# Layer 2 window attention: weights loaded first, exponentials behind the copies, routing in slots 12 to 18

## The chip, the cores and the metric

The kernel runs on one core of one Trainium2 chip. The metric is the time of one execution on the device in microseconds (us), the median of several runs; less is better. The engines are TensorE (PE, matrix products; PEld is its weight load), VectorE (DVE), ScalarE (ACT), GpSimd (POOL) and SyncE (SP, which here only asks for transfers).

## The reference

Input: two images of 256 channels and 32 x 32 pixels, float32. Four layers, each an attention and, in layers 2 and 3, a mixture of experts. Layers 0 and 1 are attentions over the pixels. Cut to the part that matters here:

```python
# layer 2, tokens t: (2, 1024, 256)
t = t + window_attention(layernorm(t))      # rolled by 32, windows of 64 tokens, 8 heads of 32:
#   qkv = x @ w_qkv.T + b_qkv; sim = q @ k.T * 32**-0.5 + rel_pos; probs = softmax(sim)
#   out = (probs @ v) @ w_out.T + b_out
# then a mixture of 8 experts, top 2 of each token, on x = layernorm(t):
logits = x @ Wr + br
top_p, top_idx = top_k(softmax(logits), 2); weights = top_p / top_p.sum()
xn = layernorm(x); xe = xn * ln_g[e] + ln_b[e]      # x is normalised a second time
y_e = gelu(xe @ W1[e] + b1[e]) @ W2[e] + b2[e]
t = t + sum over the two experts of weights * y_e
# layer 3: an additive attention (tanh) over each image, then experts again
```

## The kernel before

`Stack.run` does layer 0, layer 1, then builds `Late` (constants, small weights, the code of the experts), then `window_attention`, then `Late.run`. Tokens lie in `t`, 16 tiles of 128 tokens by 256; tiles 0 to 7 are image 0, tiles 8 to 15 image 1. A tile holds two windows.

`window_attention` loads `w_qkv`, `w_out` and the biases after `Late.__init__` has put its own loads into the same SP queue, normalises image 0 (`normed(0)`: inverse root, eight scalings, transposes into `uT`), and then runs a loop of 20 slots. In slot i stand, in this order, `value(i)` (v of the tile), `scores(i)` (32 small products, softmax on DVE, ACT and POOL, result in `probs`), `turn(i-2)` (transposes of `probs`, two copies to `ptT` on ACT), one of four parts of the q and k projection of a later group of four tiles (`project`), a step of `normed(1)` in the first six slots, `sums(i-3)` (probabilities times v), `output(i-4)` (times `w_out`, added to `t`), and from slot 10 on three steps of `route`. `route` is the generator `late.dispatch(2, 0)`: twice `gate` (statistics, normalisation, transposes and router product of four tiles), then `Late.route` (softmax, the two best experts, counts, slots of the sorted list, rows of the expert weights), a second normalisation of the eight tiles (`norm`), 16 scatters of the tokens into `slots_in` by POOL's indirect transfers (L1161), and `shift` (the experts' second bias times the weights of the token, added to `t`). What the loop has not used up of it, `Late.run` continues as step `D20`.

The loop is written inside

```python
with tc.manual_schedule(engines={engines.PE, engines.Activation}):
```

so PE and ACT work in the order of the loop's lines; DVE, POOL and SP are ordered by the framework's scheduler by readiness and program order. Products go to PSUM tiles of one pool with three buffers (`misc`, tag `ps_mm`): `ps_va`, two of `ps_pt`, `ps_qk`, `ps_wo` in each slot; a buffer is free when its reader has drained it.

Where the change touches it: the exponential L884 stands on ACT inside `scores(i)`, so ahead of the copies of `turn(i-2)` L909; v is drained by DVE with its bias (L901), q by ACT (L858), k by DVE (L860); `output` makes `y` on DVE (L935) and adds it to `t` on POOL (L936).

`Late.run` interleaves named steps by a plan: for each the steps that must have been issued before it, a planned time and the distance between its pieces. `E20` and `E21` are the experts of the two images, `D21` the routing of image 1, `C20` the collection of the results, `A0` the additive attention of image 0. `E20` needs `D20`: it loads its tokens (`xr`, L1371) from `slots_in`, and the weights of the expert (`ew`, `fetch`, L1322) by POOL's indirect transfers.

Of the kernel before, what the change touches and what calls it, by code (L numbers as in the profile page):

```python
# [27 lines left out]
P = 128  # L28
# [41 lines left out]
class Stack:  # L70
# [707 lines left out]
    def window_attention(self, t, late):  # L778
# [7 lines left out]
        with ExitStack() as ctx:  # L786
# [35 lines left out]
            uT, q, k, v, pT, o = {}, {}, {}, {}, {}, {}  # L822
# [22 lines left out]
            def project(g, part):  # L845
# [11 lines left out]
                if part < CC:  # L857
                    nc.scalar.activation(to, ps, AF.Identity, bias=b_qk[:, part : part + 1])  # L858
                else:
                    nc.vector.tensor_scalar(to, ps, b_qk[:, part : part + 1], None, ALU.add)  # L860

            def scores(i):
# [21 lines left out]
                nc.scalar.activation(l, l, AF.Exp)  # L884
# [8 lines left out]
            def value(i):  # L893
# [7 lines left out]
                nc.vector.tensor_tensor(v[i], ps, b_v, ALU.add)  # L901
# [25 lines left out]
            def output(i):  # L927
# [13 lines left out]
            engines = mybir.EngineType  # L941
            with tc.manual_schedule(engines={engines.PE, engines.Activation}):
                for part in range(2 * CC):
                    project(0, part)
                for i in range(NT + 4):
# [3 lines left out]
                    if 2 <= i < NT + 2:  # L949
                        turn(i - 2)  # L950
                    if i + 4 < NT:
                        project(i // 4 + 1, i % 4)
                    if i < 6:
                        next(other, None)
                    if 3 <= i < NT + 3:
                        sums(i - 3)
                    if 4 <= i:
                        output(i - 4)
                    if i >= 10:
                        for _ in range(3):  # L960
                            next(route, None)
# [28 lines left out]
class Late:  # L990
# [3 lines left out]
    def __init__(self, ctx, stack, t):  # L994
# [4 lines left out]
        self.early = ctx.enter_context(tc.tile_pool(name="early_sb", bufs=2))  # L999
        self.made = {}  # L1000
# [3 lines left out]
        tl = lambda name, shape: self.w.tile(shape, F32, name=name)  # L1004
        self.wr = {l: stack.load(self.w, n, "(c p) e -> p c e", p=P) for l, n in ((2, "wr"), (3, "gate_w"))}
# [138 lines left out]
    def dispatch(self, *key, done=0):  # L1144
# [3 lines left out]
        n = len(tokens)  # L1148
        for half in range(done, n // 4):
# [6 lines left out]
        nc = self.nc  # L1156
# [13 lines left out]
        if l == 2:  # L1170
            yield from self.shift(*key)
# [532 lines left out]
    def run(self, route):  # L1704
# [132 lines left out]
```

## Time and profile before

| what | us |
|---|---|
| median of 3 runs (2844.81 to 2851.49) | 2851.44 |
| the profiled execution | 2887.74 |
| its span, first to last instruction | 2886.0 |
| PE busy / DVE / ACT / POOL in the span | 2635.3 / 1944.8 / 1815.6 / 1235.5 |
| end of layer 1's last product | 1623.2 |
| first q/k product of layer 2 (L852) | 1640.5 |
| first and last scatter (L1161) start | 1779.6, 1801.6 |
| first product of the experts (L1404) starts | 1810.6 |

The profile is of one execution, which took somewhat longer than the runs timed without it; times inside it are from its first instruction. A line of the timeline gives start, duration, engine, line of the kernel, operation, `out<-in`, shapes, count, and in brackets how long the engine stood idle before and what ended that. A line of the waits gives who waited for whom, us in total, times, and the longest. In the table by stages each engine's busy time is followed by its number of instructions; PEclk is the clock granted to PE as a share of full speed.

### The profile page before, as it was taken

To read this page: it belongs to the slowest core of one execution; us is meant where nothing else is said; L and a number is where in the kernel's file an instruction comes from. 1 tells how busy PE (TensorE), PEld (TensorE's weight loads), DVE (VectorE), ACT (ScalarE), POOL (GpSimd) and SP (SyncE) were. 2 spreads that over 40 slices of the span, in tenths; PEclk is the share of its full clock that TensorE was granted. 3 is DMA by queue.
4 is the path that set the end of the run, shared out by engine and by line. 5 is a ranking of instruction groups with operands and counts; after the bars stand their busy time and mean duration, and the time that the engine had idled before them with its cause. 6 is when DMAs were issued, how large, how long until landed. Compare 5 with 4: busy or idle time off the path is not lost. (4 is left out here: it accounts for less than half of the span.)

```text
span 2886.0 us, 77396 instructions
## 1 busy us (share of the span) xinstructions
PE 2635.3 (91%) x32006; PEld 1643.6 (57%) x32006; DVE 1944.8 (67%) x3642; ACT 1815.6 (63%) x2685; POOL 1235.5 (43%) x1302
## 2 busy tenths in 40 slices
PE   7899999999999998799999686999999988999987
PEld 3455555555555555555555454998666632465676
DVE  5999999999999999478789577633422343134242
ACT  2777777778777777255555231211699878889722
POOL 4877777777777775001111134244111112102242
PEclk9999999999999999899999897999999999899998
DMA  3000000000000000111010100543222001322354
GB/s 133 3 3 3 3 3 3 3 3 3 3 3 3 3 3 3 49 31 28 11 31 9 28 1 30 202 134 99 68 81 76 16 24 35 128 67 87 116 166 125
DMA packets 180577, 131.39 MB, mean 46 GB/s; under 512 B 130992, under 2 KB 162368, under 8 KB 173056
## 3 DMA queue, kind: packets, MB, share of 16 engines
q0 software_dynamic: 29232, 81.71, 8.5%
q1 hardware_dynamic: 147824, 44.25, 6.8%
q8 instruction: 251, 4.11, 0.6%
q10 hardware_dynamic: 3168, 0.48, 0.1%
q14 instruction: 102, 0.84, 0.1%
HBM read 181.24 MB, written 29.49 MB: 73 GB/s over the span
## 5 line engine op out<-in xcount | busy, mean ns | idle before, releaser
L188 ACT ACTIVATE sc<-sc,sa_shift 128x1024 f32<-128x1024 f32 x512 | 584.5, 1144 | 153.1 <-DMA sa_shift<-sa_min 150.8
L201 DVE STREAM_TRANSPOSE wt<-sc 128x1024 f32<-128x1024 f32 x512 | 601.5, 1207 | 0.2 <-ACT sc L188 0.2
L1622 ACT ACTIVATE th<-kT,qb 128x1024 f32<-128x1024 f32 x512 | 540.4, 1135 | 66.2 <-PE ps_e L1631 40.1
L211 PEld LDWEIGHTS ps_o<-wt,v 128*64 128x64 f32 x8192 | 444.4, 137 | 188.9 <-issue 106.2
L143 PE MATMUL ps_s<-kT,qT 64*32 64x512 f32 x8192 | 527.6, 595 | 18.0 <-ACT sc L153 17.2
L211 PE MATMUL ps_o<-wt,v 128*64 128x128 f32 x8192 | 505.0, 276 | 26.8 <-DVE oT L372 26.7
L166 POOL TENSOR_TENSOR fold<-sc 128x512 f32<-128x512 f32 x256 | 329.2, 1286 | 195.9 <-ACT sc L153 177.0
L168 POOL TENSOR_TENSOR fold<-sc,fold 128x512 f32<-128x512 f32 x256 | 328.4, 1283 | 21.4
L153 ACT COPY sc<-ps_s 128x1024 f32<-128x1024 f32 x256 | 256.0, 1000 | 111.0 <-PE ps_s L143 57.1
L1631 PE MATMUL ps_e<-th,pick 128*32 128x512 f32 x2048 | 305.7, 613 | 20.5 <-ACT th L1622 9.3
L1404 PEld LDWEIGHTS ps_h<-xe,ew 128*128 128x128 f32 x2320 | 278.1, 194 | 63.6 <-issue 39.0
L150 DVE TENSOR_SCALAR_CACHE_REDUCE sc<-ps_s 128x1024 f32<-128x1024 f32 x256 | 304.3, 1189 | 7.1 <-PE ps_s L143 6.6
L1404 PE MATMUL ps_h<-xe,ew 128*128 128x128 f32 x2320 | 295.0, 281 | 13.7 <-issue 5.6
L1424 PE MATMUL ps_y<-ew,h 128*128 128x256 f32 x1160 | 275.6, 387 | 8.2 <-ACT h L1410 5.6
L143 PEld LDWEIGHTS ps_s<-kT,qT 64*32 64x32 f32 x8192 | 134.4, 106 | 230.2 <-issue 163.4
L1424 PEld LDWEIGHTS ps_y<-ew,h 128*128 128x128 f32 x1160 | 215.6, 193 | 66.7 <-issue 23.0
L630 ACT ACTIVATE sc<-sc,l_least 128x1024 f32<-128x1024 f32 x128 | 146.7, 1147 | 125.8 <-DVE sc L617 125.5
L1415 DVE TENSOR_TENSOR hb<-ps_h,ew 128x512 f32<-128x512 f32 x115 | 79.4, 691 | 207.3 <-PE ps_h L1404 167.1
L1428 DVE COPY y<-ps_y 128x256 f32<-128x256 f32 x99 | 41.9, 423 | 229.7 <-PE ps_y L1424 209.9
L1393 ACT ACTIVATE h<-hb 128x512 f32<-128x512 f32 x115 | 71.5, 623 | 193.0 <-DVE hb L1415 173.7
L636 DVE STREAM_TRANSPOSE wt<-sc 128x1024 f32<-128x1024 f32 x128 | 153.3, 1225 | 46.0 <-ACT sc L630 25.4
L617 DVE TENSOR_SCALAR_CACHE_REDUCE sc<-ps_s 128x1024 f32<-128x1024 f32 x128 | 150.7, 1213 | 40.3 <-PE ps_s L609 40.2
(286 smaller groups left out, 3139.1 us busy)
## 6 DMA issues: line engine op xcount, KB each, us to landing
xr<-slots_in SPq DMA_DIRECT2D x99, 128.0 KB
slots_out<-y SPq DMA_DIRECT2D x99, 128.0 KB
sa_got<-sa_least SPq DMA_DIRECT2D x512, 0.5 KB
sa_shift<-sa_min SPq DMA_DIRECT2D x512, 0.2 KB
slots_in<-zero POOLq DMA_DIRECT2D x46, 128.0 KB
kh<-kh SPq DMA_DIRECT2D x32, 128.0 KB
qh<-qh SPq DMA_DIRECT2D x32, 128.0 KB
sa_sums<-sa_total SPq DMA_DIRECT2D x244, 1.0 KB
```

The costliest lines, as they stand in the source:

```text
L143: nc.tensor.matmul(ps[r][S * c : S * (c + 1), a, :].rearrange("p (b i) -> p b i", i=S), lhsT=qT[half, p, S * i : S * (i + 1)], rhs=keys[ha ...
L150: nc.vector.tensor_scalar(scores[m][0], flat[0], 1.0, None, ALU.mult, ALU.min, accum_out=least[m // 2][:, 0, h : h + 1])
L153: nc.scalar.copy(scores[m][1], flat[1])
L166: nc.gpsimd.tensor_tensor(y, a, b, ALU.subtract)
L168: nc.gpsimd.tensor_tensor(y, a, y, ALU.subtract)
L188: nc.scalar.activation(scores[m][r], scores[m][r], AF.Exp, bias=shift[m // 2][:, r : r + 1], scale=-1.0, accum_out=total[i][:, 2 * p + r, ...
L201: nc.vector.transpose(weights[i, h][:, 2 * p + r, :], x)
L211: nc.tensor.matmul(sums[i][64 * k : 64 * (k + 1)], lhsT=v[:, at % NT, 64 * (at // NT) : 64 * (at // NT + 1)], rhs=weights[i, h][:, :, S * ...
L1404: nc.tensor.matmul(ps[:, j, :], lhsT=a[:, c, at : at + P], rhs=x[:, c, :], start=(c == 0), stop=(c == CC - 1),)
L1424: nc.tensor.matmul(ps, lhsT=h[:, j, :], rhs=w2[:, j, :], start=(j == 0), stop=(j == HB - 1))
L1622: nc.scalar.activation(h, keys, AF.Tanh, bias=self.qb[b][:, s // G, g : g + 1])
L1631: nc.tensor.matmul(pe[i][c * U : (c + 1) * U, a, :], lhsT=self.pick[:, k, :], rhs=h[:, a, :], start=(k == 0), stop=(k == G - 1),)
```

## The change

- The weights and biases of the window attention are loaded by `Late.__init__`, ahead of all its other loads, into one tile `front` (two tiles of weights side by side); `kT` of the additive attention later uses the same tile. The tiles `loaded` for the expert weights move from the pool made in `Late.run` to the one of `Late.__init__`.
- The bias of v leaves the loop: `output_shift` multiplies it by `w_out` once and adds it to `b_out`. v and k are drained by ACT.
- `scores` is cut in three: up to the subtraction in place, the exponential (`weigh`) behind `turn`, and the sum, reciprocal and products (`divide`) behind `sums`.
- `output` adds the product straight into `t` on DVE; `b_out` is added to `t` by POOL two slots after the tile's scores.
- The steps of `route` stand in slots 8, 9 and 12 to 18, half of a slot's steps ahead of `output`, half behind. All 32 steps that remain are used in the loop.
- The second normalisation uses the first one's variance (variance times the square of the inverse root) instead of new statistics, and scales on ACT, ahead of `Late.route`. For image 0 the first two weight fetches are issued ahead of the scatters. `shift` becomes the steps `B20` and `B21` of the plan.

```diff
@@ window_attention
-            w_qkv = self.load(w, "w_qkv", "(c p) o -> p c o", p=P)
-            w_out = self.load(w, "wa_w_out", "(c p) o -> p c o", p=P)
-            b_qk = self.load(w, "b_qk")
-            b_v, b_out = self.load_row(w, "b_v"), self.load_row(w, "wa_b_out")
+            w_qkv, w_out, b_qk, b_v, b_out = late.windows
...
+            spread = w.tile([P, CC, P], F32, name="spread")
+            nc.gpsimd.tensor_copy(spread, broadcast(b_v, [P, CC, P]))
+
+            def output_shift():
+                ps = late.misc([P, C], "ps_wo")
+                for c in range(CC):
+                    nc.tensor.matmul(
+                        ps, lhsT=spread[:, c, :], rhs=w_out[:, c, :], start=(c == 0), stop=(c == CC - 1)
+                    )
+                nc.vector.tensor_tensor(b_out, b_out, ps, ALU.add)
...
-                if part < CC:
-                    nc.scalar.activation(to, ps, AF.Identity, bias=b_qk[:, part : part + 1])
-                else:
-                    nc.vector.tensor_scalar(to, ps, b_qk[:, part : part + 1], None, ALU.add)
+                nc.scalar.activation(to, ps, AF.Identity, bias=b_qk[:, part : part + 1])
...
-                nc.scalar.activation(l, l, AF.Exp)
+                weights[i] = l, m, rec
+
+            def weigh(i):
+                nc.scalar.activation(weights[i][0], weights[i][0], AF.Exp)
+
+            def divide(i):
+                l, m, rec = weights.pop(i)
                 nc.vector.tensor_reduce(m, l, AX.X, ALU.add)
...
-                nc.vector.tensor_tensor(v[i], ps, b_v, ALU.add)
+                nc.scalar.copy(v[i], ps)
...
-                y = sb.tile([P, C], F32, name="y")
-                nc.vector.tensor_tensor(y, ps, b_out, ALU.add)
-                nc.gpsimd.tensor_tensor(t[:, i, :], t[:, i, :], y, ALU.add)
+                nc.vector.tensor_tensor(t[:, i, :], t[:, i, :], ps, ALU.add)
...
+            pieces = {8: 2, 9: 2, 12: 4, 13: 6, 14: 6, 15: 4, 16: 3, 17: 3, 18: 2}
             with tc.manual_schedule(engines={engines.PE, engines.Activation}):
                 for part in range(2 * CC):
                     project(0, part)
+                output_shift()
                 for i in range(NT + 4):
                     if i < NT:
                         value(i)
                         scores(i)
                     if 2 <= i < NT + 2:
                         turn(i - 2)
+                    if i < NT:
+                        weigh(i)
                     if i + 4 < NT:
                         project(i // 4 + 1, i % 4)
                     if i < 6:
                         next(other, None)
+                    if 2 <= i < NT + 2:
+                        nc.gpsimd.tensor_tensor(t[:, i - 2, :], t[:, i - 2, :], b_out, ALU.add)
                     if 3 <= i < NT + 3:
                         sums(i - 3)
+                    if i < NT:
+                        divide(i)
+                    for _ in range(pieces.get(i, 0) // 2):
+                        next(route, None)
                     if 4 <= i:
                         output(i - 4)
-                    if i >= 10:
-                        for _ in range(3):
-                            next(route, None)
+                    for _ in range((pieces.get(i, 0) + 1) // 2):
+                        next(route, None)
@@ Late.__init__
+        self.loaded = [
+            [self.w.tile([P, WIDE], F32, name=f"ew{run}{k}") for k in range(2)] for run in range(LANES[2])
+        ]
...
+        self.front = self.w.tile([P, 2 * N], F32, name="front")
+        weights = []
+        for name, cols in (("w_qkv", slice(0, 3 * C * CC)), ("wa_w_out", slice(3 * C * CC, 4 * C * CC))):
+            weights.append(self.front[:, cols].rearrange("p (c o) -> p c o", c=CC))
+            nc.sync.dma_start(out=weights[-1], in_=self.ins[name].rearrange("(c p) o -> p c o", p=P))
+        self.windows = (
+            *weights, stack.load(self.w, "b_qk"), stack.load(self.w, "b_v", "(c p) -> p c", p=P),
+            stack.load_row(self.w, "wa_b_out"),
+        )
@@ scale
+        self.last_norm = mv, rs
@@ dispatch
+        again = self.early.tile([P, n], F32, name="again", bufs=1) if l == 2 else None
         for half in range(done, n // 4):
             yield from self.gate(l, b, half)
-        yield from self.route(key, n)
+            if l == 2:
+                mv, rs = self.last_norm
+                to = again[:, 4 * half : 4 * half + 4]
+                nc.vector.tensor_tensor(to, mv[:, :, 1], rs, ALU.mult)
+                nc.vector.tensor_tensor(to, to, rs, ALU.mult)
         u = self.u[key]
         if l == 2:
-            yield from self.norm(lambda i: u[:, i, :], lambda i: u[:, i, :], range(n))
+            rs = self.inverse_root(again, 1e-5)
+            yield 3.0
+            for i in range(n):
+                nc.scalar.activation(u[:, i, :], u[:, i, :], AF.Identity, scale=rs[:, i : i + 1])
+            yield 5.0
+        yield from self.route(key, n)
         p, shares, slots, rows = self.routes[key]
+        if key == (2, 0):
+            self.fetch(key, 0)
+            self.fetch(key, 0, 1)
...
-        if l == 2:
-            yield from self.shift(*key)
@@ Late.project
-            self.kT[b] = self.sb.tile([P, N], F32, name="kT")
+            self.kT[b] = self.front[:, b * N : (b + 1) * N]
@@ Late.run
-        self.loaded = [
-            [self.sb.tile([P, WIDE], F32, name=f"ew{k}", bufs=LANES[2]) for k in range(2)] for _ in range(LANES[2])
-        ]
...
+            "B20": (self.shift(2, 0), ("D20",), 100, 5.0),
+            "B21": (self.shift(2, 1), ("D21",), 215, 6.0),
...
-            "C20": (self.collect(2, 0), ("E20",), 172, 2.0),
+            "C20": (self.collect(2, 0), ("E20", "B20"), 172, 2.0),
...
-            "C21": (self.collect(2, 1), ("E21",), 456, 2.0),
+            "C21": (self.collect(2, 1), ("E21", "B21"), 456, 2.0),
```

More of the change, by code (lines that the diff above doesn't have):

```diff
@@ L820, in window_attention @@
                 nc.gpsimd.memset(x, 0.0)
-            uT, q, k, v, pT, o = {}, {}, {}, {}, {}, {}
+            uT, q, k, v, pT, o, weights = {}, {}, {}, {}, {}, {}, {}
+            spread = w.tile([P, CC, P], F32, name="spread")
[7 more added lines that the diff above has]
+                nc.vector.tensor_tensor(b_out, b_out, ps, ALU.add)
             def normed(b):
@@ L1148, in dispatch @@
         n = len(tokens)
+        nc = self.nc
+        again = self.early.tile([P, n], F32, name="again", bufs=1) if l == 2 else None
         for half in range(done, n // 4):
             yield from self.gate(l, b, half)
-        yield from self.route(key, n)
+            if l == 2:
[3 more added lines that the diff above has]
+                nc.vector.tensor_tensor(to, to, rs, ALU.mult)
         u = self.u[key]
         if l == 2:
-            yield from self.norm(lambda i: u[:, i, :], lambda i: u[:, i, :], range(n))
+            rs = self.inverse_root(again, 1e-5)
[4 more added lines that the diff above has]
+        yield from self.route(key, n)
         p, shares, slots, rows = self.routes[key]
-        nc = self.nc
+        if key == (2, 0):
+            self.fetch(key, 0)
+            self.fetch(key, 0, 1)
         before = []
```

## The prediction

> **What bounds the kernel now.** I read the table of 40 slices first (72 us each). TensorE (PE) is lowest in the 23rd to 25th, 1587 to 1803 us: 6, 8 and 6 tenths.
>
> ```profile
> PE   7899999999999998799999686999999988999987
> ```
>
> Layer 2's attention lies there (1623 to 1809), so next I read the busy time of its stages.
>
> ```profile
> core 0: us, PE busy (x) PEld busy (x) DVE busy (x) ACT busy (x) POOL busy (x), PEclk, DMA share, GB/s
> 1640.00:1734.00 94.00, 79.55 (x793) 48.89 (x794) 63.19 (x136) 25.73 (x51) 30.14 (x32) 0.94 0.03 6
> 1734.00:1787.00 53.00, 35.84 (x364) 25.81 (x363) 43.82 (x164) 10.84 (x24) 17.77 (x20) 0.81 0.03 11
> 1787.00:1810.00 23.00, 11.40 (x33) 7.15 (x33) 8.95 (x34) 0.00 (x0) 18.34 (x20) 0.51 0.41 148
> 1810.00:2000.00 190.00, 189.66 (x1299) 176.84 (x1298) 88.04 (x256) 34.86 (x53) 67.97 (x68) 0.99 0.41 141
> ```
>
> Four regimes: slots 0 to 11 of the attention loop, PE 85% busy; slots 12 to 19 with the routing, PE 68%, VectorE (DVE) 83%; a stretch in which only GpSimd (POOL) works at the scatters; then the layer 2 experts, PE full. Whatever brings the experts' start (first `ps_h` at 1810.6) forward counts in full; PE work pushed behind it is paid in full. The waits of PE in the first of these stages:
>
> ```profile
> PE ps_wo L931 <- ACT ptT L909: 7.5, 6, 2.0
> PE ps_qk L852 <- DMA sb_w_qkv<-in_w_qkv: 6.2, 1, 6.2
> PE ps_tr L840 <- ACT ptT L909: 4.5, 3, 2.4
> PE ps_qk L852 <- DVE va L901: 1.1, 2, 0.7
> ```
>
> 12.0 us for ScalarE's (ACT) copies of the turned probabilities, 6.2 for the weights. The copies are late because ACT works in the loop's order, and the exponential of the same slot stands in front of them:
>
> ```profile
> ACT l L884 <- DVE l L883: 59.8, 12, 6.7
> ACT l L884 <- DVE ir_a L1078: 14.0, 1, 14.0
> ```
>
> The timeline shows the ends that matter: weights asked for late, the slots known, first and last scatter, first expert input.
>
> ```profile
> 1635.81 0.38 SPq L85 DMA_DIRECT2D sb_w_qkv<-in_w_qkv  x1
> 1640.51 8.84 PE L852 MATMUL ps_qk<-uT,sb_w_qkv 128*128 128x512 f32 x16 [6.23 <-DMA sb_w_qkv<-in_w_qkv]
> ...
> 1779.40 0.16 DVE L1266 CAST rt_slot<-rt_one 128x8 uint32<-128x8 f32 x1
> 1779.64 1.20 POOL L1161 DMA_INDIRECT slots_in<-u,rt_slot  x1 [0.87 <-DVE latest L1290]
> ...
> 1801.60 0.97 POOL L1161 DMA_INDIRECT slots_in<-u,rt_slot  x1 [0.30 <-issue]
> 1804.15 21.95 SPq L1371 DMA_DIRECT2D xr<-slots_in  x7
> ```
>
> **What the Trainium skill says.** "TensorE: Matmul & The Clock Gate", Part 1: after about 3.4 us without work the array runs at half rate. The trace agrees: the four records of a value product span 1.03 us in slot 4 and 2.02 in slot 15, granted clock 0.81. "SBUF — State Buffer", Who interferes with whom: a DVE operation with two SBUF inputs and a POOL operation that reads SBUF exclude each other. It agrees: the subtraction L883, 0.69 alone, took 1.56 and 1.51 beside POOL's L889. "ScalarE: Activation LUTs", Table sets: copy and identity are in every table set, so those moved to ACT add no table load; before, only L1393 and L1210 show loads (1.28 us each).
>
> **The change, part by part.**
>
> *Weights first.* `w_qkv` and `w_out` head SP's queue when layer 1 lets go of its memory, at 1623.3 (`sb_wr` starts there now), and took 4.6 us to land (1635.8 to 1640.4): there by 1629. The projections then wait for the transposed input only, whose last transposes end at 1634.3. Gain 6.2, less one new product, `output_shift`, of four matmul records as in a `ps_wo` (1.1) ahead of slot 0: 5.0. Its `spread` copy on POOL (about 0.7, as L936) and one add on DVE (0.4) lie beside the projections. Queued behind the weights on SP: some 20 small loads, then `turned`, asked for at 1637.3 now. SP waits for earlier loads to land now and then (1.1 us on `sb_br`, 0.7 on `sb_l_ln` in the waits of its queue) and will do so on `w_qkv`; I take `turned` to be 1.5 to 2 us later, without 1 MB beside it. The bias was ready at 1644.8 and scores(0) will end at about 1645.5: nothing if that holds, up to 3 us lost if not.
>
> *Copies ahead of exponentials.* Slot 0 to slot 12 (first value product of each) is 1648.8 to 1733.7 = 84.9. Removed: 12.0 on `ptT`, and 1.6 on `va` and `y` (buffers drained by DVE), as the value copy goes to ACT. Added: the router of the first half, 1.85, which comes in slot 9 instead of 12. That is 73.1. PE's work agrees: a full slot is 1.03 + 0.49 + 1.10 + 1.98 + 0.65 + 1.13 = 6.4. ACT now holds per slot 0.38 (value), 2 x 0.58, 0.63, 0.69 (q or k), 0.38 = 3.2 of 6.4. A q/k product sits behind exp(i) in one of three PSUM buffers, which the next slot's second half needs; the exponential may start some 2.8 us late before PE feels it. I allow 2.4 for new stalls (bounds 0 and 10): 75.5. So slot 12 starts 5.0 + 9.4 = 14.4 earlier, at 1719.3.
>
> DVE loses 16 value adds (0.42) and 8 k biases (0.75), 12.7 in all, partly hidden; `y` becomes an add straight into `t` at the same 0.42, and POOL's `t` add (0.73) becomes the add of `b_out`, no longer between output(7) and the statistics.
>
> *Route.* From slot 12 to the slots known is 1733.7 to 1779.4 = 45.7, DVE idle for only some 6 of it: DVE decides. Removed: the second normalisation, 8 statistics (0.41), 8 aggregates (0.17), 8 scalings (0.51) = 8.7, and four value adds 1.6; added four small products, 0.8. POOL's hop of 0.9 and the first router's 1.8 go too. 45.7 - 8.7 - 1.6 + 0.8 - 0.9 - 1.8 = 33.5. The 8 scalings now stand on ACT in slot 13, 8 x about 0.4 = 3.2 as L925: behind them wait the route's Exp, the next value copy and the `ptT` copies. I count them at nothing while DVE's chain is longer; without that cover they cost 3. Bounds: 25 (route takes DVE first) and 42 (DVE keeps the old interleaving).
>
> *Fetch before scatters.* POOL must first have the rows (about 1.5 after the slots), then issues two weight fetches, 2 x 1.3, then the 16 scatters as before. Plus 4.1. Their 2.1 MB, at the 259 GB/s seen between 1800 and 1830, drain in 8 us while the scatters take 20 to issue: nothing more, at worst 8. From last scatter to first `ps_h`, 9.0 us, I leave as it is; that the weights are there earlier gains nothing, since `ps_h` waits for the scattered input.
>
> Sum at the experts' start: 5.0 + 9.4 + 12.2 - 4.1 = 22.5 earlier, 1788 for 1810.6.
>
> *What is pushed back.* `shift(2,0)` leaves the gap at 1791 to 1806 for the experts' stage, where PE is full: 2 x (1.0 + 3.8) at half clock, half of that at full clock = 4.8 lost (bounds 0 and 9.6). `shift(2,1)` moves from one full stage to another: nothing. `C20` now also waits for `B20`, which starts at planned time 100 and ends by 140, before 172: no wait. Its DVE adds (0.69) lie beside PE there. On the other side the gap could now take image 1's transposes and routers (1.0 + 1.85 per half): 0 to 6 gained, taken as 0. `kT` in the weights' place and `loaded` in another pool add no instruction; before, the fetch already followed the scatters on POOL, so the pool was no wait.
>
> Sum: 22.5 - 4.8 = **17.7 us faster**. The profiled execution took 2887.7 (span 2886.0), 36 above the median of 2851.4; I take the same step off both: 2870 and **2834**.
>
> **Rivals.**
> *ACT becomes the bound (slower).* All copies out of PSUM but the `t` adds stand in one in-order queue with an exponential that DVE releases; each microsecond by which DVE is late past the 2.8 of slack returns to PE in that slot. For: exponentials waited 59.8 and once 14.0 us for DVE. Against: DVE is only 67% busy in slots 0 to 11 and loses work. It needs 17.7 + 8.6 = 26 us, or 2.2 in each of 12 slots, to end slower; at 3 a slot: 2870.
> *DVE's order keeps the route long (no change).* Only PE and ACT follow the loop; DVE and POOL are ordered by the framework. With the route at 45 as now, 14.4 - 4.1 - 4.8 = 5.5 remain: 2846. For: DVE is the saturated engine there, and image 1's statistics were mixed in.
> *The gap fills up (much faster).* Route at 25 instead of 33.5 and 5 of image 1's PE work in the gap: 31 faster, 2820. For: the pieces are dense in slots 13 and 14. Against: each is a dependent chain of 0.2 us steps.
> *The weights do not come early*, because their new place is released no sooner: 5 less, 2839.
>
> **How the numbers follow.** A measurement of this kernel tells about 0.3%, 8.6 us, from no change. My forecast, with the late weights in it, 0.57; filled gap 0.20; long route 0.15; ACT bound 0.08. Faster 0.77, same 0.15, slower 0.08. The range of 8 in 10 goes from 2812 (filled gap with the lower bounds) to 2850 (long route with some stalls).
>
> **What would show it.** First `ps_qk` near 1634.5; waits of `ps_wo` on `ptT` gone; slot 12 near 1719; slots known near 1753; last scatter near 1779; first `ps_h` near 1788; `ps_b` inside the full stage. I am wrong if PE waits for q, k or value copies by more than 1 us a slot, if the first `ps_h` comes after 1800, or if the experts' stage grows by more than 10.

## The result, and the profile after

The kernel after takes 2838.6 us (median of 8 runs, 2832.6 to 2841.0), the kernel before 2851.5 beside it (8 runs, 2844.8 to 2853.0). The ratio is **0.9959, 95% interval 0.9951 to 0.9968**: 11.7 us faster, 14.0 to 9.1 by the interval, where 17.7 were forecast. The profiled execution of after took 2838.2, span 2836.5.

The profile of before that the prediction reads was of an execution 36 us above its median. The experiments below show why: it has the extra waits of another chip, none of them ahead of 1780 us. So the two traces are compared up to the first `ps_h` only, and times there are counted from **one mark: the end of layer 1's last value product `ps_o`**, 1613.9 in before and 1613.1 in after. That takes out what executions differ by up to then: over all profiles the mark lies between 1610.7 and 1615.2.

The row of 40 slices (71 us each now). The 23rd to 25th read 7, 8, 6 and were 6, 8, 6:

```profile
PE   7899999999999999699999786899999999999997
```

Busy time by stage, from the first q/k product to slot 12, to the slots known, to the first expert product, and on:

```profile
core 0: us, PE busy (x) PEld busy (x) DVE busy (x) ACT busy (x) POOL busy (x), PEclk, DMA share, GB/s
1633.00:1719.00 86.00, 76.91 (x796) 48.81 (x796) 57.96 (x131) 36.69 (x72) 35.50 (x38) 0.94 0.04 7
1719.00:1758.00 39.00, 26.24 (x284) 20.07 (x283) 31.32 (x114) 11.56 (x27) 8.30 (x8) 0.74 0.00 1
1758.00:1796.00 38.00, 21.48 (x134) 16.30 (x133) 21.32 (x92) 4.05 (x9) 24.24 (x24) 0.65 0.48 169
1796.00:1986.00 190.00, 189.65 (x1295) 177.07 (x1295) 80.69 (x221) 36.86 (x61) 71.23 (x72) 0.99 0.40 131
```

The loop's first twelve slots are now 89% PE (85% before). From slot 12 to the slots known it is 39.3 us instead of 45.7, and PE is busy for 67% of it. The 38 us from there to the first expert product hold 21.5 us of PE work, of which more below. The experts' stage is full, as it was.

The waits of these first slots (engine, line, what it waited for: us in total, times, longest):

```profile
ACT l L893 <- DVE l L889: 13.5, 9, 6.4
...
PE ps_pt L920 <- POOL probs L901: 4.9, 1, 4.9
PE ps_va L910 <- ACT qh L866: 1.5, 1, 1.5
PE ps_wo L943 <- ACT qh L866: 1.2, 1, 1.2
```

PE's waits for `ptT` are gone, and ACT's exponentials wait 13.5 us for DVE's subtraction where in the same slots of before it is 54.2 (the 59.8 that the prediction shows are of all slots). New is 4.9 us for POOL's probabilities. The timeline's ends, in the order of those shown of before (start, duration, engine, line, operation, tiles, and the idle time ahead with what ended it):

```profile
1622.22 0.39 SPq L1034 DMA_DIRECT2D front<-in_w_qkv  x1
...
1632.93 7.03 PE L861 MATMUL ps_qk<-uT,front 128*128 128x512 f32 x16
...
1758.57 0.16 DVE L1314 CAST rt_slot<-rt_one 128x8 uint32<-128x8 f32 x1
...
1758.77 1.11 POOL L1211 DMA_INDIRECT slots_in<-u,rt_slot  x1 [8.89 <-DVE rt_slot L1314]
...
1786.79 0.97 POOL L1211 DMA_INDIRECT slots_in<-u,rt_slot  x1 [0.30 <-issue]
...
1795.64 4.21 PE L1452 MATMUL ps_h<-xe,ew 128*128 128x128 f32 x18 [0.61 <-DVE xe L1431]
```

| us behind the mark | before | predicted | after |
|---|---|---|---|
| first `ps_va` (slot 0) | 35.1 | 30.1 | 27.6 |
| slot 12 | 119.6 | 105.2 | 106.2 |
| slots known | 165.3 | 139 | 145.5 |
| last scatter | 187.5 | 165 | 173.7 |
| first `ps_h` | 196.8 | 174 | 182.6 |

(Before is from its second profile, `before_again`; it agrees with the first to 0.3 us in each row. Predicted is the prediction's own times and savings, set against this mark.) Slot 12 came where it was expected, by two errors that cancel. From slot 12 to the slots known half of the saving came that was counted on, and the scatters cost more.

### The profile page after: what moved, and what is told of

Its sections match the earlier page's. It is cut to its first block, busy times and chain, and to the rows that moved or that the text cites. A ratio compares the mean times of both kernels' runs of the same rounds, so it can differ in the third digit from the quotient of the medians.

```text
span 2836.5 us, 77376 instructions
## 1 busy us (share of the span) xinstructions
PE 2619.5 (92%) x32010; PEld 1643.1 (58%) x32010; DVE 1925.6 (68%) x3579; ACT 1830.9 (65%) x2723; POOL 1237.0 (44%) x1303
## 5 line engine op out<-in xcount | busy, mean ns | idle before, releaser
L1670 ACT ACTIVATE th<-front,qb 128x1024 f32<-128x1024 f32 x512 | 539.9, 1134 | 51.4 <-PE ps_e L1679 45.3
L211 PEld LDWEIGHTS ps_o<-wt,v 128*64 128x64 f32 x8192 | 444.2, 137 | 188.0 <-issue 106.2
L1679 PE MATMUL ps_e<-th,pick 128*32 128x512 f32 x2048 | 297.6, 607 | 5.8 <-DVE sc_a L1686 4.4
```

What stands on the lines that cost most here:

```text
L211: nc.tensor.matmul(sums[i][64 * k : 64 * (k + 1)], lhsT=v[:, at % NT, 64 * (at // NT) : 64 * (at // NT + 1)], rhs=weights[i, h][:, :, S * ...
L1670: nc.scalar.activation(h, keys, AF.Tanh, bias=self.qb[b][:, s // G, g : g + 1])
L1679: nc.tensor.matmul(pe[i][c * U : (c + 1) * U, a, :], lhsT=self.pick[:, k, :], rhs=h[:, a, :], start=(k == 0), stop=(k == G - 1),)
```

## The experiments

Each kernel is the kernel after with one edit, unless said otherwise. The first four ran on a chip where the kernel before takes 2882.7 us instead of 2848 to 2851, so their ratios belong to that chip; what I read from them across chips are the marks up to the slots known, ahead of the first of the extra waits (1768.5, in u_exp). These marks agree on both: the same kernel, as u_shift and u_shift_2, has slot 12 at 106.1 and 106.2 and the slots known at 145.4 and 145.5.

**u_weights**: the weights late again.

```diff
-        self.front = ...            # and the loads of the windows' weights and biases
         self.wr = ...
         ...
         self.ba = stack.load_row(self.w, "ba")
+        self.front = ...            # the same lines, at the end of SP's loads
```

> The kernel after with one part undone: the layer 2 weights and biases are asked for at the end of SP's loads instead of at their head. My theory (the parts' gains add, because PE follows its own order and everything behind slot 0 moves with it): first ps_qk back by 6 us, from 1632.9 to about 1639, slot 12 and the first ps_h back by 5 to 6, the time about 2844 (ratio to before 0.9978). Rival (another input holds slot 0 anyway, such as the relative position bias or the transposed input): slot 0 moves by less than 2 us and the time stays at 2839 to 2840.

Measured: ratio 1.0014 (1.0008 to 1.0021); slot 0 at 35.7 instead of 27.6, slot 12 at 113.4, slots known at 152.5. So the early weights are worth **8.1 us at slot 0 and 7 at the slots**, more than I had. That the time is above before's on this chip was expected by neither theory; the kernel after itself was not run there, so the edit's effect on the time cannot be given.

**u_exp**: the exponential ahead of the copies again.

```diff
                         scores(i)
+                        weigh(i)
                     if 2 <= i < NT + 2:
                         turn(i - 2)
-                    if i < NT:
-                        weigh(i)
```

> The kernel after with one part undone: in ACT's order each slot's exponential again stands ahead of the copies of the turned probabilities. My theory: the 12 us of waits of the output product for those copies return, slots 0 to 12 take about 86 us instead of 78.6, slot 12 starts 7 to 9 later, the route takes its 39 from there, the time about 2846 (0.998). Rival (DVE and POOL set the pitch of slots 0 to 12 once the value copy and the k bias have left DVE): slots 0 to 12 stay within 3 us of 78.6, the time 2839 to 2841.

Measured: ratio 0.9999 (0.9988 to 1.0010). PE's waits for `ptT` in the stretch to slot 12:

```profile
PE ps_tr L849 <- ACT ptT L921: 2.6, 3, 0.9
PE ps_wo L943 <- ACT ptT L921: 2.4, 5, 1.4
...
PE ps_tr L1142 <- ACT ptT L921: 0.9, 1, 0.9
```

5.9 us of waits return, not 12, and slots 0 to 12 take 81.7 us instead of 78.6: 3.1. By parts, slots 3 to 9 take 39.7 instead of 34.4, and slots 9 to 12 take 21.5 instead of 23.7. The rival's bound (within 3 us) is missed by little and my 7 to 9 by far, though the rival's reason does not hold either: in slots 3 to 9 the order is worth 5.3.

**u_shift** and, on the other kind of chip, **u_shift_2**: the shift behind the scatters again.

```diff
             yield None if l == 2 else 0.5
+        if key == (2, 0):
+            yield from self.shift(*key)
...
-            "B20": (self.shift(2, 0), ("D20",), 100, 5.0),
```

> The kernel after with one part undone: the shift of image 0 (weights times the second bias, added to the tokens) stands again directly behind its scatters instead of in the experts' stage. My theory: its products run in the gap before the first ps_h, where PE has at least 3 us free, and the experts' stage loses 4.8 us of PE work: about 2834 (0.994), first ps_h where it was, within 2 us. Rival (the gap is full: transposes and routers of image 1 already run there): what the shift takes in the gap pushes one of those back into the experts' stage or the first ps_h later by 3 to 6 us, and the time stays at 2838 to 2840.

> The same kernel as u_shift (shift of image 0 directly behind its scatters), again, since that run fell on a chip with the long waits that nothing releases, where the gap ahead of the first ps_h can't be read. On a chip without them: if the shift's products fit beside image 1's routers in the gap, the first ps_h stays within 1 us of the kernel after (182.6 us behind layer 1's last product) and the time falls by the 4.8 that I put on the shift in the full stage, to about 0.994. Rival (the gap is full): the first ps_h moves back by 3 to 6 us, or a router of image 1 leaves the gap, and the time is the same as the kernel after's within 2 us (0.9955).

Measured: 0.9970 (0.9958 to 0.9982) where the chip has the extra waits, **0.9951 (0.9939 to 0.9962)** where not. In the second the first `ps_h` is at 182.9, where it was; but the shift's products take PE from 1780.1 to 1789.1, one half of image 1 gets half its transposes in ahead of the first `ps_x`, and both routers, which the kernel after has in this gap, come behind it. The rival holds: the gap is full, and what goes in pushes something else out. From the first `ps_h` on the profile is 3.4 us shorter than after's, but that stretch runs from 1036 to 1042 us over kernels in which the shift has the place that it has in after, so this is no measurement of the shift.

**before_again**: the kernel before, for a second profile.

> The kernel before, unchanged, for a second profile: the first took 2887.7 us where the median is 2851.4. My theory: the 36 us are single stalls behind 2000 us of that execution (ACT stood for 13 us around 2450 with seven weight fetches under way), so that this profile spans about 2850 and agrees with the first within 2 us up to the first additive product (2055); all that the change did is then seen ahead of 1811. Rival: the stalls belong to the kernel before and are part of what the change removes: they return here, at the same places.

Measured: 2884.4 median, span 2885.1, ratio 1.0003 (0.9993 to 1.0012). My theory is wrong as written: the extra time is no single execution's. The rival has it that the waits return, in part at the same places, but they are not the kernel's: the kernels of u_weights, u_exp and u_shift, which have the change, show them on this chip too, and `after_again` shows none. The waits of this profile for which no releasing instruction is found:

```profile
ACT th L1622 <- remote: 11.0, 6, 3.7
...
DVE y L1428 <- remote: 6.9, 1, 6.9
```

With 9.6 and 7.2 on DVE's `hb` and `t` and 3.8 each on its `xe` and POOL's `ew` they are 42 us, all behind 1880 us. The sizes differ from the first profile's: ACT `th` 11.0 instead of 17.6, DVE `y` 6.9 instead of 16.3. Some places return, as DVE `t` at 2715, 7.2 and 7.3 us.

**after_again**: the kernel after, unchanged, with a second profile.

> The kernel after, unchanged, a second profile beside the kernel before. The four kernels of the first call, run together, showed waits of 2 to 10 us, 30 to 60 us a run, for which the profile names no releasing instruction ('<-remote'), behind 1780 us, where weights are fetched; the profile of before that I predicted from has them too, the one of after has none. My theory: they belong to the chip that a kernel happens to run on, not to the kernel. If this run lands on that kind of chip, before takes about 2882 and this profile has such waits too, 30 us or more, with the same times as the first profile of after up to the slots (first slot cast 145 us behind layer 1's last product); the ratio is then 0.994 to 0.999. If not, before takes about 2851, no such wait shows, ratio 0.996. Rival: the change itself removes the waits (its fetches ahead of the scatters, the weights' new place); then before takes 2882 and this kernel 2838, ratio 0.985.

Measured: 2835.5 beside 2847.8, ratio **0.9954 (0.9940 to 0.9968)**. The profile has no wait of that kind, as none of the nine profiles from where before takes 2848 to 2851 has. Kernels with the change (the first three) have them on the other chip. So they go with the chip, or with the time at which it was used, since each chip was used once; the change does not remove them. All five marks of the table repeat to 0.1 us.

**late_scale**: the eight scalings behind the route's exponential.

```diff
             rs = self.inverse_root(again, 1e-5)
             yield 3.0
-            for i in range(n):
-                nc.scalar.activation(u[:, i, :], ..., scale=rs[:, i : i + 1])
-            yield 5.0
-        yield from self.route(key, n)
+        for k, wait in enumerate(self.route(key, n)):
+            yield wait
+            if l == 2 and k == 2:      # behind the route's Exp
+                for i in range(n):
+                    nc.scalar.activation(u[:, i, :], ..., scale=rs[:, i : i + 1])
+                yield 5.0
```

> The kernel after with the eight scalings of the tokens on ACT moved behind the route's exponential. In the profile of after that exponential ran 8.7 us behind its input, with the eight scalings (3.3 us) directly ahead of it in ACT's queue. My theory: DVE's chain had slack for part of it, so the slots are known 2 to 3 us earlier and the time falls by 2 to 3 us against the kernel after (ratio about 0.995). Rival one (DVE alone decides the route): the slots move by less than 1 us, the time not at all. Rival two (the framework's order of DVE changes with it): any shift between 3 us earlier and 5 later, with another order of DVE's instructions.

ACT's timeline, in the kernel after and then in this one:

```profile
1740.55 3.31 ACT L1200 ACTIVATE u<-u,ir_y 128x256 f32<-128x256 f32 x8
1743.76 0.24 ACT L1258 ACTIVATE rt_lg<-rt_lg 128x64 f32<-128x64 f32 x1
```

```profile
1741.40 0.26 ACT L1260 ACTIVATE rt_lg<-rt_lg 128x64 f32<-128x64 f32 x1
1741.56 3.29 ACT L1203 ACTIVATE u<-u,ir_y 128x256 f32<-128x256 f32 x8
```

The exponential runs 3.2 us earlier from slot 12, and the slots are known 0.8 earlier. Ratio 0.9963 (0.9949 to 0.9976), the same as after's. The prediction's cover over the scalings was there: 3.3 us on ACT cost the slots less than 1, and the time nothing that these runs can tell.

**u_norm**: the second normalisation by statistics on DVE again.

```diff
-            rs = self.inverse_root(again, 1e-5)     # and the eight scalings on ACT
+            yield from self.norm(lambda i: u[:, i, :], lambda i: u[:, i, :], range(n))
         yield from self.route(key, n)
```

> The kernel after with one part undone: the second normalisation of image 0's and image 1's tokens is done by statistics, aggregates and scalings on DVE again (8.7 us of DVE per image), at the place of the scalings. If DVE decides the route, as I predicted: slots known 6 to 9 us later, less 3 for the scalings that no longer stand ahead of the route's exponential on ACT: 3 to 6 us longer than the kernel after (about 0.998). Rival (ACT's queue decides): the slots come within 2 us of the kernel after's or earlier, the time the same within 2 us.

DVE in the stretch from slot 12 to the slots (third pair of columns):

```profile
core 0: us, PE busy (x) PEld busy (x) DVE busy (x) ACT busy (x) POOL busy (x), PEclk, DMA share, GB/s
1717.00:1759.00 42.00, 27.29 (x287) 20.89 (x287) 35.46 (x133) 9.03 (x21) 8.31 (x8) 0.76 0.01 1
```

It is busy for 35.5 of 42 us, against 31.3 of 39 in after. The slots come at 147.8, 2.3 later, the first `ps_h` at 187.3, 4.7 later. Ratio 0.9970 (0.9958 to 0.9981), beside 0.9954 for after: some 4 us by the ratios, 1.8 by the medians, and the intervals overlap, so that it is not clear of noise. At the slots the rival is about right and DVE's work is not what decides; at the first `ps_h` my 3 to 6 is.

**u_fetch**: the two weight fetches behind the scatters again.

```diff
-        if key == (2, 0):
-            self.fetch(key, 0)
-            self.fetch(key, 0, 1)
```

> The kernel after with one part undone: the two weight fetches come behind the scatters again. My theory: POOL issues its scatters 2.6 us sooner, the last one ends 2 to 3 us earlier, and the first ps_h follows 2 us earlier because it waits for the scattered input or for image 1's router and not for the weights: 2 us faster than the kernel after (0.9952). Rival one (the weights land last): the fetch now ends about 8 us behind the last scatter and the first ps_h waits for it, 2 to 4 us slower than the kernel after. Rival two: POOL's order around the last probabilities decides, no difference within 1 us.

Measured: last scatter at 168.1 instead of 173.7, first `ps_h` at 178.9 instead of 182.6, ratio 0.9964 (0.9950 to 0.9977): no gain in the time that these runs can tell. At the first `ps_h` my theory has the direction right, and rival one is wrong; the scatters gain 5.6 us, more than the fetches' 2.6. PE's waits from slot 9 to the first `ps_h`:

```profile
PE ps_pt L920 <- POOL probs L901: 9.0, 1, 9.0
PE ps_counts L1279 <- DVE rt_eq L1272: 7.6, 1, 7.6
PE ps_x L1424 <- DMA xr<-slots_in: 6.1, 1, 6.1
```

PE's wait for the last probabilities has grown to 9.0 from 7.0, because POOL now runs nine scatters ahead of them, and 6.1 us are lost on the scattered input itself. PE's order is written down before the run, and in this one it has the transposes and the beginning of the router of one half of image 1 ahead of `ps_x`, where the kernel after has both halves. So part of the 3.7 us is work that comes later.

**u_drains**: value and k products drained by DVE again.

```diff
-                nc.scalar.activation(to, ps, AF.Identity, bias=b_qk[:, part : part + 1])
+                if part < CC: ...                   # q as it was
+                else:
+                    nc.vector.tensor_scalar(to, ps, b_qk[:, part : part + 1], None, ALU.add)
...
-                nc.scalar.copy(v[i], ps)
+                nc.vector.tensor_copy(v[i], ps)
```

> The kernel after with one part undone: the value products are drained by DVE again (a copy, as long as the add it replaces) and the k products by DVE with their bias. Measured from layer 1's last product, slots 0 to 12 fell from 84.5 us to 78.6; putting the exponentials back ahead of the copies gave only 3.1 of these 6 back. My theory now: the rest belongs to the drains, so slots 0 to 12 take about 81 to 82 here and slot 12 starts 3 us later; the time about 2 to 4 us above the kernel after (0.997). Rival (ACT has the slack and DVE too: the two halves of the gain belong together): slots 0 to 12 within 1 us of 78.6, the time the same.

Measured: slots 0 to 12 take 78.8 us against 78.6; ratio 0.9965 (0.9951 to 0.9978). The rival holds; my theory does not. Which engine drains these products makes no difference here by itself that can be told.

**u_pieces**: the steps of the route placed as before.

```diff
-                    for _ in range(pieces.get(i, 0) // 2):
-                        next(route, None)
                     if 4 <= i:
                         output(i - 4)
-                    for _ in range((pieces.get(i, 0) + 1) // 2):
+                    for _ in range(3 if i >= 10 else 0):
                         next(route, None)
```

> The kernel after with one part undone: the steps of the route are taken as in the kernel before, three a slot from slot 10 on, all behind the slot's output product. My theory: the route is a chain on an in-order DVE whose order the placing of the steps decides, more than the amount of work (returning 8 us of statistics to DVE moved the slots by only 2): with three steps a slot it takes about 46 as in the kernel before, slots known 5 to 8 us later than in the kernel after, the time 3 to 6 us above it (0.998). Rival (the amount of work on DVE decides): the slots move by less than 2 us.

Measured: 2824.3 beside 2848.8, ratio **0.9918 (0.9905 to 0.9930)**. Both theories were wrong, and in sign: undoing this part makes the kernel 10 to 12 us faster than after (0.9918 beside 0.9954 and 0.9959), the fastest of all that ran. The slots are known at 143.5, 2.0 earlier. PE's waits from slot 9 to the first `ps_h` give the likely reason. In the kernel after:

```profile
PE ps_tr L1143 <- DVE u L1132: 8.0, 4, 3.5
PE ps_counts L1282 <- DVE rt_eq L1275: 7.6, 1, 7.6
PE ps_pt L920 <- POOL probs L901: 7.0, 1, 7.0
```

In u_pieces, over the same stretch:

```profile
PE ps_counts L1280 <- DVE ir_a L1109: 5.9, 1, 5.9
...
PE ps_x L1425 <- DMA xr<-slots_in: 4.3, 1, 4.3
```

In both PE waits for the route's counts, but what stands behind the waiting instruction differs. In the kernel after the counts have their place in slot 14:

```profile
1750.88 0.66 PE L1282 MATMUL ps_counts<-rt_eq,before 128*128 128x64 f32 x2 [7.56 <-DVE rt_eq L1275]
...
1751.76 2.02 PE L943 MATMUL ps_wo<-front,oT 128*128 128x256 f32 x4
1753.57 1.91 PE L910 MATMUL ps_va<-front,uT 128*128 128x256 f32 x4
1755.41 0.53 PE L877 MATMUL ps_s<-kh,qh 32*64 32x64 f32 x32
...
1765.43 1.03 POOL L901 TENSOR_TENSOR probs<-l,wa_rec 64x512 f32<-64x512 f32 x1
```

For 7.6 us PE stands at `ps_counts`, and value and score products of slot 15, which need nothing of the route, stand behind it. They run at 1753.6 and 1755.4, after which DVE and ACT have their share, and when slot 15's division is ready POOL has begun the scatters: it runs at 1765.4, and its second half 4.6 us later. The wait itself is not new. The kernel before has it in the same place, with slot 15's value product behind it, but there the division still came ahead of the first scatter (1779.6):

```profile
1767.37 0.69 PE L1234 MATMUL ps_counts<-rt_eq,before 128*128 128x64 f32 x2 [7.54 <-DVE rt_eq L1227]
...
1776.62 2.15 POOL L889 TENSOR_TENSOR probs<-l,wa_rec 64x512 f32<-64x512 f32 x2 [0.37 <-DVE rt_lg L1263]
```

In u_pieces:

```profile
1736.10 0.49 PE L877 MATMUL ps_s<-kh,qh 32*64 32x64 f32 x32
...
1745.14 0.66 PE L1280 MATMUL ps_counts<-rt_eq,before 128*128 128x64 f32 x2 [5.89 <-DVE ir_a L1109]
...
1753.49 2.00 PE L943 MATMUL ps_wo<-front,oT 128*128 128x256 f32 x8
...
1741.99 2.15 POOL L901 TENSOR_TENSOR probs<-l,wa_rec 64x512 f32<-64x512 f32 x2 [2.54 <-DVE rt_one L1263]
1754.36 1.10 POOL L1209 DMA_INDIRECT slots_in<-u,rt_slot  x1 [10.22 <-DVE rt_slot L1312]
...
1776.44 0.97 POOL L1209 DMA_INDIRECT slots_in<-u,rt_slot  x1 [0.30 <-issue]
...
1770.03 3.82 PE L1170 MATMUL ps_router<-sb_wr,uT 128*128 128x8 f32 x16
...
1785.10 3.14 PE L1450 MATMUL ps_h<-xe,ew 128*128 128x128 f32 x16
```

Slot 15's scores run at 1736.1 and its division at 1742.0, 12 us ahead of the first scatter; the wait for the counts comes at a place where only turns, sums and outputs are left. The attention's last product ends at 1755.5, 144.8 behind the mark, against 165.6. Image 1's second router is done 11 us before the first `ps_h` and the scatters are not interrupted: 22.1 us from first to last, with the fetches in them, against 28.0. The first `ps_h` is at 174.4, 8.2 earlier. The route is not shorter: 40.6 us from slot 12 against 39.3; but slot 12 itself is 3.4 earlier, since in the kernel after the first half's router stands in slot 9, which takes 10.6 us. How the 8.2 divide between this router and the place of the counts is read from the traces; no run moved one without the other. The 2 to 4 us by which the time falls further than the first `ps_h` moved are not traced.

**gap_order**: a version meant to beat both.

```diff
-        if key == (2, 0):                           # no fetches ahead of the scatters
-            ...
-                    nc.gpsimd.tensor_tensor(
+                    (nc.vector if i == NT - 1 else nc.gpsimd).tensor_tensor(
                         probs[i % RING][rows, :, rows], ...
...
+                for _ in range(8):                  # image 1: transposes and routers,
+                    next(second, None)              # in PE's written order
-            return route
+            return route, second
```

> A version meant to beat both: the kernel after without the two fetches ahead of the scatters, with the last slot's division on DVE instead of POOL (there it stood behind 9 scatters, and PE waited 9.0 us for it in u_fetch, 7.0 in the kernel after), and with both transposes and routers of image 1 placed by PE's written order at the end of the attention loop, ahead of the first expert product. My theory: PE leaves the attention 8 us earlier, both routers end before the scattered tokens land, the last scatter ends about 169 us behind layer 1's last product (173.7 in after, 168.1 in u_fetch) less 2 for the divisions, and the first ps_h starts at about 176 instead of 182.6: 5 to 7 us faster than the kernel after (0.9935). Rival (landing of scatters and weights decides): first ps_h at 178 as in u_fetch, 2 to 3 us faster (0.995).

Measured: 2828.5 beside 2848.8, ratio **0.9932 (0.9918 to 0.9946)**: about 7 us faster than after. The last scatter starts at 165.4, the first `ps_h` at 174.7, as my theory had it or earlier. PE's timeline at the end of the attention:

```profile
1768.37 1.99 PE L943 MATMUL ps_wo<-front,oT 128*128 128x256 f32 x8
...
1783.29 3.16 PE L1175 MATMUL ps_router<-sb_wr,uT 128*128 128x8 f32 x14 [0.26 <-DVE uT L1147]
1786.73 0.69 PE L1427 MATMUL ps_x<-ident,xr 128*128 128x128 f32 x2 [0.28 <-DVE rt_lg L1179]
```

The last output ends at 1770.4, 8.5 us earlier from the mark than in after; both routers end before the first `ps_x`, and that waits for no transfer. That slot 15's division no longer meets the scatters on POOL is seen in the trace: PE no longer waits for the last probabilities. How much each of the three edits brings to the time was not separated. Its slot 14 still has the wait of 7.6 us for the counts, which u_pieces avoids. A kernel with both was not run.

## Why the prediction was right, and where it was not

The sign and the range were right, and the path: what decides is when the first `ps_h` starts, and what is pushed behind it. Its terms, in order:

- **Weights first: 5.0 predicted, 7.5 at slot 0.** The mechanism is as described; u_weights takes 8.1 away again. Of the surplus, 0.3 is an earlier first `ps_qk` and 2.1 the stretch from there to slot 0: 7.7 us, new product included, where 8.7 and 1.1 were taken. Before, PE came out of 6.3 us without work and its first products took up to 1.19 us each; now all 16 take 0.59, and the granted clock of the stretch is 1.00 instead of 0.79. The clock belonged into this step. The feared delay of the bias came: slot 0's scores ended at 1642.1 and DVE took them at 1645.1. PE lost 1.0 to it in slot 1, and a part of the 4.9 of the next point.
- **Copies ahead of exponentials: 9.4 predicted, 6.0.** In slots 3 to 9, 9.2 went, and the waits for `ptT` with them; u_exp shows that the order accounts for 5.3 of these, u_drains that the drains account for none, and what brought the other 3.9 is open. Slots 9 to 12 gave 2.8. But slots 0 to 3 grew by 6.0, and this I had costed at nothing. POOL's add of `b_out`, which I took as one per slot "no longer between output(7) and the statistics", was put by the framework in one block of 16 ahead of everything (below: DVE's reciprocal of slot 0, POOL, PE):

```profile
1650.90 0.20 DVE L898 RECIPROCAL wa_rec<-wa_m 128x8 f32<-128x8 f32 x1
...
1641.37 12.23 POOL L971 TENSOR_TENSOR t<-t,sb_wa_b_out 128x256 f32<-128x256 f32 x16 [10.26 <-DVE sb_wa_b_out L831]
1653.55 4.82 POOL L901 TENSOR_TENSOR probs<-l,wa_rec 64x512 f32<-64x512 f32 x4
...
1656.21 1.97 PE L920 MATMUL ps_pt<-ident,probs 128*128 128x128 f32 x8 [4.91 <-POOL probs L901]
```

  Slot 0's division was ready at 1651.1 and started at 1653.6, behind the block; PE waited 4.9, of which these 2.5 are the block's directly. The rest is DVE's delay ahead of it: the bias landed at about 1642.8, behind slot 0's scores, and its copies (L807, L809) took 2.4 us beside the block, where in before they took 0.9. u_weights separates the two. There the bias was copied by 1644.4 and slot 0's scores ended at 1652.1; its division was ready at 1656.3 and still ran behind the block (POOL, PE):

```profile
1651.38 12.32 POOL L971 TENSOR_TENSOR t<-t,sb_wa_b_out 128x256 f32<-128x256 f32 x16 [8.48 <-DVE sb_wa_b_out L831]
1663.66 4.36 POOL L901 TENSOR_TENSOR probs<-l,wa_rec 64x512 f32<-64x512 f32 x4
...
1665.87 1.97 PE L920 MATMUL ps_pt<-ident,probs 128*128 128x128 f32 x8 [7.36 <-POOL probs L901]
```

  So the block alone can hold PE for 7.4 us. No run took the block away. I had allowed 2.4 for new stalls; PE's four largest new waits before slot 12 are 8.6 together. The two errors, +2.5 and -3.4, explain why slot 12 came within 1 us: that is luck.
- **Route: 12.2 predicted, 6.4.** The step that failed is "DVE decides": I subtracted all of DVE's removed work from the route's length. u_norm put 8.7 of that work back, and took the 3.3 of scalings off ACT, and the slots moved by 2.3; late_scale gave ACT's exponential 3.2 us and the slots moved by 0.8. The route is a chain through PE, ACT and DVE, and each of them takes it in a queue with attention work; in after 15.3 us go to the second router, 9.2 to the exponential, 14.8 to the slots. My rival "DVE's order keeps the route long" had the outcome half right and the engine wrong: the order that hurts is PE's, which stands for 7.6 us at the counts (7.5 in before) and 4.9 at the second half's transposes (part of the 8.0 above).
- **Fetch before scatters: 4.1 predicted, 6.0.** u_fetch shows 5.6 of it go with the fetches. Their own 2.6 us was right. The 1.5 for the rows did not come, since four scatters run ahead of the first fetch. The rest is slot 15's division: it takes POOL away from the scatters and fetches for 5.9 us (1765.4 to 1771.4), 3.6 of them idle for no reason that the profile shows, against 2.9 in u_fetch. The prediction named POOL's queue for the fetches but not the probabilities of slot 15 as standing in it.
- **Last scatter to the first `ps_h`: 9.0 predicted, 8.9.**
- **Pushed back: 4.8 for the shift, less 0 for a filled gap.** The first `ps_h` came 14.2 us earlier and the time fell by 11.7 to 13.1 (two ratios), so 1.1 to 2.5 were paid behind it. The reading that fits is that image 1's second transpose and both routers ran in the gap, 4.7 us at full clock (1.0 + 2 x 1.85), against the shift's 4.8. That work is in the gap is shown, the 4.8 is not: u_shift_2 changed the time by less than can be told.
- **`C20` behind `B20`, and the ACT-bound rival:** PE's waits for q, k or value copies in slots 0 to 12 sum to 2.7 us, far from 1 a slot, and in u_drains ACT's share of the drains costs nothing that can be told.
- **Readings of the profile that were off:** the stretch of the scatters is not one in which only POOL works, since PE is busy there for 11.4 of 23 us in the line that the prediction shows; the value product in slot 4 took 1.13 us (1.03 is slot 5's); and over the whole execution of before five more lines have table loads. None of this changes a sum: up to the first expert product neither kernel has a table load in layer 2.

In sum, 26.6 were expected at the slots and 19.8 came; 22.5 at the first `ps_h` and 14.2 came; 17.7 in the time and about 12 came. Undoing the placing of the route's steps alone gives 22.4 at the first `ps_h`, nearly what I had predicted for the whole. So the missing 8 us can be had back by that one part, whose steps I had put at about nothing: 1.85 for the router added ahead of slot 12, 1.8 taken off the route. That the two figures meet is luck as well: the single terms differ.

## What to carry to other kernels

Where an engine's order is written by hand, a step that waits for another engine costs what stands behind it, so place it behind all work that is already free to run, not where its turn comes soonest; a dense placing of a chain does not shorten it if other queues set its pace. Work that is left to a scheduler on another engine (here the adds and divisions on POOL) must be looked up in the order that it actually got, since sixteen small adds in one block stood ahead of the one division that PE waited for. And a stage's gain is best measured from a mark close ahead of it, and its cause by undoing one part at a time: the sum of a change can be right while one part of it works against it.

## What the runs showed of the hardware

The kernel before takes 2882.7 us on one chip and 2848 to 2851 on others, steady to 0.3% on each. On the slower one the profile shows waits of up to 10 us that no recorded instruction ends, on ACT, DVE and POOL, 42 us in the profile of before_again and none in those from the others. Up to the slots known the two agree (u_shift and u_shift_2, to 0.1 us from the mark); behind them, where the tokens are scattered and the expert weights fetched (131 GB/s in the experts' stage of after), they part. What releases these waits stays open.

POOL's division again lengthened short DVE operations: the comparison of 64 elements in a row (L1266 of the kernel after) took 0.23 us at 1745.7 and 1.11 at 1747.7, beside POOL's division at that time. This agrees with the Trainium skill, "SBUF — State Buffer", Who interferes with whom: a DVE operation with two SBUF inputs and a POOL operation that reads SBUF exclude each other, and the one that comes second waits until the first is through. Here the short one took nearly five times its own length.
